# Projections of a two-layer graph network on one Trainium2 core: normalizing and turning the next 512 rows ahead of emptying the current products, and values before the weights' product

## The chip, the core and the metric

The kernel runs on one core of a Trainium2 chip. The metric is device time in microseconds (us) of one execution; the kernel before was timed three times. The engines go by the profile's names: PE is TensorE's matmul, PEld its weight load, DVE is VectorE, ACT is ScalarE, POOL is GpSimd, SP is SyncE, which here only issues transfers.

## What is computed

`x` has 4096 rows of 512, `adj` is a 4096 x 4096 matrix. Layer 0 is attention over all rows with the adjacency added to the scores; layer 1 is graph attention with 8 heads.

```python
h = relu(layernorm(x))
q, k, v = h @ Wq.T + bq, h @ Wk.T + bk, h @ Wv.T + bv
x = x + softmax(q @ k.T / sqrt(512) + adj + adj) @ v
h = relu(layernorm(x))
x = x + gat(h, adj)      # 8 heads of 64, masked softmax, elu
```

The change touches only how `h`, `v` and the queries of layer 0 are made. The kernel doesn't make `k`: it multiplies the two weights into one 512 x 512 matrix once (`a_sb`) and keeps a column `c_sb` from the query bias, so that the scores are a product of `h` with "queries" which already hold both weights.

## The kernel before, in words

`fast_path` has three stages: projections (pool `proj`, lines 168 to 260), attention of layer 0 (pool `attn`, 262 and following) and graph attention. A second path, taken only if a flag asks for it, plays no part here.

The projections start with loads: the first 512 rows of `x` by SyncE, then Wv, the bias rows, Wq and Wk by ScalarE's queue. The two weights share one buffer (`raw`, line 231), so Wk is loaded when Wq has been turned. Each is turned with 16 transposes on TensorE (line 237), four to one PSUM buffer (tag `pt`, two buffers), which ScalarE copies out (238). Their product takes 16 matmuls (242), the bias column 16 more with one moving column (250).

Then a loop over 8 sets of 512 rows (`NS`, lines 255 to 260), and in each turn:

- `load_x`: one transfer of 1 MB for the set after this one, into one of two `xt` buffers.
- `hidden`: the statistics of the four blocks of 128 rows on VectorE (156, 157), the reciprocal root through a power on GpSimd (144) and four small VectorE steps (145 to 148), the normalization in place (187), 16 transposes on TensorE into two `pt` buffers (194), and ScalarE's relu from there into `hT` (195).
- `values_of`: four products of four matmuls each into `mm` buffers (201; four of them), each emptied by VectorE, which adds the bias (205).
- `queries`: four more such products with the weights' product as stationary side (215), emptied and scaled by VectorE into `qs` (219), and a store of 1 MB to DRAM by SyncE (222).

float32 matmuls show as two in the profile, so the 16 matmuls of values are "x32" there.

Each engine works through its own queue in order. `seq(...)` keeps an instruction at its place in program order; where it is missing, a scheduler may place the instruction by its own judgement. In `hidden`, the VectorE work is under `seq`, the TensorE and ScalarE work is not; the emptying instructions at 205 and 219 aren't either. Waits between engines are semaphores that the framework sets where a tile is written or read.

When the last queries have been stored, the pool closes and the attention stage takes its space; its first loads (328, 266, 337) wait for that.

Of the kernel before, what the change touches and what calls it, by code (L numbers as in the profile page):

```python
# [10 lines left out]
F32 = mybir.dt.float32  # L11
BF16 = mybir.dt.bfloat16
AF = mybir.ActivationFunctionType
# [5 lines left out]
P = 128  # L19
N = 4096  # L20
D = 512
# [3 lines left out]
SB = 4  # L25
NS = NB // SB
KC = D // P
# [8 lines left out]
GC = 512  # L36
# [10 lines left out]
@with_exitstack  # L47
def adj_preln_gnn_kernel(
    ctx: ExitStack,
    tc: tile.TileContext,  # L50
    x: bass.AP,
    adj: bass.AP,
    wqT: bass.AP,
    bq: bass.AP,
    wkT: bass.AP,
    bk: bass.AP,
    wvT: bass.AP,
    bv: bass.AP,
    w1: bass.AP,
    a1T: bass.AP,  # L60
    a2T: bass.AP,
    a_ln: bass.AP,
    b_ln: bass.AP,
    out: bass.AP,
):
    nc = tc.nc
    keep = ctx.enter_context(tc.tile_pool(name="keep", bufs=1))
    flag = keep.tile([1, 1], mybir.dt.int32, name="flag")
    fast_path(
        tc, flag, x, adj, wqT, bq, wkT, bk, wvT, bv, w1, a1T, a2T, a_ln, b_ln, out  # L70
    )

    low = nc.values_load(flag[0:1, 0:1])
    with tc.If(low > 0):
        general_path(tc, x, adj, wqT, bq, wkT, bk, wvT, bv, w1, a1T, a2T, a_ln, b_ln, out)
# [3 lines left out]
def fast_path(  # L79
# [18 lines left out]
    nc = tc.nc  # L98
    seq = tc.keep_in_program_order
# [4 lines left out]
    ident = const.tile([P, P], F32, name="ident")  # L104
# [46 lines left out]
    def layernorm_stats(pool, rows, name):  # L151

        st = pool.tile([P, SB, 6], F32, name=f"{name}st", tag=f"{name}st", bufs=2)
        mv = pool.tile([P, SB, 2], F32, name=f"{name}mv", tag=f"{name}mv", bufs=2)
        for b in range(SB):
            seq(nc.vector.bn_stats(st[:, b, :], rows[b]))
            seq(nc.vector.bn_aggr(mv[:, b, :], st[:, b, :]))
        v = pool.tile([P, SB], F32, name=f"{name}v", tag=f"{name}v", bufs=2)
        seq(nc.vector.tensor_scalar_add(v, mv[:, :, 1], LN_EPS))
        return mv, rsqrt(pool, v, [P, SB], name)  # L160


    with tc.tile_pool(name="kv", bufs=1) as kv:
        hT = kv.tile([P, KC, N], F32, name="hT")
        v = kv.tile([P, NB, D], F32, name="v")


        with tc.tile_pool(name="proj_c", bufs=1) as pc, tc.tile_pool(
            name="proj", bufs=2
        ) as work, tc.tile_pool(name="proj_ps", bufs=2, space=PSUM) as psum:  # L170
            wv_sb = pc.tile([P, KC, D], F32, name="wv_sb")
            a_sb = pc.tile([P, KC, D], F32, name="a_sb")
            c_sb = pc.tile([P, KC], F32, name="c_sb")
            bq_sb = pc.tile([P, KC], F32, name="bq_sb")
            bv_sb = pc.tile([P, D], F32, name="bv_sb")

            def load_x(sb):
                xt = work.tile([P, SB, D], F32, name="xt", tag="xt", bufs=2)
                nc.sync.dma_start(
                    out=xt, in_=x[ts(sb, SB * P), :].rearrange("(c p) d -> p c d", p=P)  # L180
                )
                return xt

            def hidden(sb, xt):
                mv, rstd = layernorm_stats(work, [xt[:, b, :] for b in range(SB)], "h")
                for b in range(SB):
                    seq(nc.vector.tensor_scalar(
                        xt[:, b, :], xt[:, b, :], mv[:, b, 0:1], rstd[:, b : b + 1],
                        ALU.subtract, ALU.mult,
                    ))  # L190
                for k in range(KC):
                    pt = psum.tile([P, 512], F32, name="pt", tag="pt", bufs=2)
                    for b in range(SB):
                        nc.tensor.transpose(pt[:, ts(b, P)], xt[:, b, ts(k, P)], ident)  # L194
                    nc.scalar.activation(hT[:, k, ts(sb, GC)], pt, AF.Relu)

            def values_of(sb):
                for b in range(SB):
                    pv = psum.tile([P, 512], F32, name="pv", tag="mm", bufs=4)
                    for k in range(KC):  # L200
                        nc.tensor.matmul(  # L201
                            pv, hT[:, k, ts(sb * SB + b, P)], wv_sb[:, k, :],
                            start=k == 0, stop=k == KC - 1,
                        )
                    nc.vector.tensor_add(v[:, sb * SB + b, :], pv, bv_sb)


            half_scale = 0.5 / math.sqrt(D)

            def queries(sb):  # L210
                qs = work.tile([P, KC, GC], F32, name="qs", tag="qs", bufs=2)
                for o in range(KC):
                    pq = psum.tile([P, 512], F32, name="pq", tag="mm", bufs=4)
                    for k in range(KC):
                        nc.tensor.matmul(  # L215
                            pq, a_sb[:, k, ts(o, P)], hT[:, k, ts(sb, GC)],
                            start=k == 0, stop=k == KC - 1,
                        )
                    nc.vector.tensor_scalar(
                        qs[:, o, :], pq, c_sb[:, o : o + 1], half_scale, ALU.add, ALU.mult  # L220
                    )
                nc.sync.dma_start(out=q_d[sb], in_=qs)

            xts = {0: load_x(0)}
            nc.scalar.dma_start(out=wv_sb, in_=wvT.rearrange("(k p) o -> p k o", p=P))
            nc.scalar.dma_start(out=bv_sb, in_=bv[None, :].to_broadcast([P, D]))
            nc.scalar.dma_start(out=bq_sb, in_=bq.rearrange("(k p) -> p k", p=P))
            with tc.tile_pool(name="proj_a", bufs=1) as pa:
                turned = {}
                for name, w in (("q", wqT), ("k", wkT)):  # L230
                    raw = pa.tile([P, KC, D], F32, name="raw", tag="raw", bufs=1)
                    nc.scalar.dma_start(out=raw, in_=w.rearrange("(k p) o -> p k o", p=P))
                    turned[name] = pa.tile([P, KC, D], F32, name=f"w{name}_t")
                    for o in range(KC):
                        pt = psum.tile([P, 512], F32, name="pw", tag="pt", bufs=2)
                        for k in range(KC):
                            nc.tensor.transpose(pt[:, ts(k, P)], raw[:, k, ts(o, P)], ident)
                        nc.scalar.copy(turned[name][:, o, :], pt)
                for k in range(KC):
                    pa_ps = psum.tile([P, 512], F32, name="pa", tag="mm", bufs=4)  # L240
                    for o in range(KC):
                        nc.tensor.matmul(  # L242
                            pa_ps, turned["q"][:, o, ts(k, P)], turned["k"][:, o, :],
                            start=o == 0, stop=o == KC - 1,
                        )
                    nc.scalar.copy(a_sb[:, k, :], pa_ps)
                for e in range(KC):
                    pcb = psum.tile([P, 1], F32, name="pcb", tag="mm", bufs=4)
                    for o in range(KC):
                        nc.tensor.matmul(  # L250
                            pcb, turned["k"][:, o, ts(e, P)], bq_sb[:, o : o + 1],
                            start=o == 0, stop=o == KC - 1,
                        )
                    nc.vector.tensor_copy(c_sb[:, e : e + 1], pcb)
            for sb in range(NS):
                if sb + 1 < NS:
                    xts[sb + 1] = load_x(sb + 1)
                hidden(sb, xts.pop(sb))
                values_of(sb)
                queries(sb)  # L260

        with tc.tile_pool(name="attn", bufs=2) as work, tc.tile_pool(
            name="attn_ps", bufs=2, space=PSUM
# [6 lines left out]
            for t, a in ((aa[0], a1T), (aa[1], a2T)):  # L270
                nc.scalar.dma_start(
                    out=t.rearrange("p h e -> p (h e)"), in_=a[None, :].to_broadcast([P, D])
# [49 lines left out]
            raws, turned, probs, queries_of, sums, rows_of, totals = {}, {}, {}, {}, {}, {}, {}  # L322
# [262 lines left out]
    with tc.tile_pool(name="ga", bufs=2) as work, tc.tile_pool(name="ga_ps", bufs=2, space=PSUM) as psum:  # L585
# [187 lines left out]
        for k in range(NS):  # L773
            nX.append(gat.tile([P, SB, NH, HD], F32, name=f"nX{k}"))
            nc.scalar.dma_start(
                out=nX[k].rearrange("p b h e -> p b (h e)"),
                in_=nX_d[k * SB : (k + 1) * SB].rearrange("b p d -> p b d"),
# [457 lines left out]
```

## Time and profile before

The three runs took 4520.41, 4521.9 and 4522.26 us, median 4521.9. The profiled execution spans 4519.6 us.

| engine | busy us | share of the span |
|---|---|---|
| PE | 4147.6 | 92% |
| DVE | 2999.3 | 66% |
| ACT | 1899.9 | 42% |
| POOL | 1844.8 | 41% |

| stretch (us) | what | length | PE busy | PE clock |
|---|---|---|---|---|
| 0 to 47.04 | weights turned and multiplied | 47.04 | 24.79 | 0.99 |
| 47.04 to 86.36 | first 512 rows | 39.32 | 32.67 | 0.84 |
| 86.36 to 360.64 | seven more sets | 274.28 | 223.68 | 0.89 |
| 360.64 to 378.3 | last store, loads of the next stage | 17.66 | 1.09 | 0.59 |
| 378.3 to 2310 | attention | 1931.70 | 1931.66 | 1.00 |
| 2310 to 4519.6 | graph attention | 2209.60 | 1933.70 | 0.97 |

How to read it: the first table is a mean over stages, and can't say where TensorE waits. The second cuts the span by stage; the difference of length and busy is the time in which TensorE did nothing. "PE clock" is the share of TensorE's full clock that was granted. An engine that is idle costs time only where it is the one that the others wait for.

In the page, a digit in the 40 slices is the busy share in tenths. In the chain of waits each line is one piece of the work that ended last, followed back from the end; "issue" is time in which the engine waited for nothing that the profile shows. In the timeline, the bracket at the end of a line tells how long the engine stood idle before it and what released it.

### The profile page before, as it was taken

The page shows a single profiled execution, that of the slowest core. Times are in us where ns is not written, and L with a number is a line of the kernel's source. Part 1 is how long each engine was busy: PE and PEld are TensorE (multiplying, and loading weights), DVE is VectorE, ACT ScalarE, POOL GpSimd, SP SyncE. Part 2 cuts the span into 40 slices and gives each one's busy share as a digit, 9 for nine tenths or more (in the row PEclk, how much of TensorE's full clock was granted, in tenths as well). Part 3 has the DMA queues.
Part 4 walks back from the last instruction along what each step waited for, and adds up shares of the span by engine and source line. Part 5 has one row for each costly group of instructions (what it writes and reads, how often), then busy time and mean ns, then how long its engine had stood idle before and what let it go on. Part 6 is the DMA issues. An engine that isn't in the chain of part 4 may idle for free.

```text
span 4519.6 us, 44777 instructions
## 1 busy us (share of the span) xinstructions
PE 4147.6 (92%) x14738; PEld 1632.5 (36%) x14890; DVE 2999.3 (66%) x4369; ACT 1899.9 (42%) x1813; POOL 1844.8 (41%) x1494
## 2 busy tenths in 40 slices
PE   6888999999999999999992799999999999999997
PEld 3333444444444444444441222222222222222222
DVE  1232234444444444444444899999999999999998
ACT  1001111111111111111110677777777777777776
POOL 0001122222222222222222566666666666666665
PEclk9889999999999999999996899999999999999999
DMA  2103233333333333333322443434444444444332
GB/s 77 56 37 118 93 103 105 115 99 119 100 102 111 100 121 100 110 100 120 98 81 104 152 134 127 131 121 131 127 127 126 129 127 132 126 128 133 123 120 70
DMA packets 486416, 501.05 MB, mean 111 GB/s; under 512 B 42144, under 2 KB 355744, under 8 KB 485152
## 3 DMA queue, kind: packets, MB, share of 16 engines
q1 hardware_dynamic: 478592, 484.67, 33.2%
q10 hardware_dynamic: 7584, 13.44, 0.8%
q8 instruction: 119, 1.95, 0.2%
q14 instruction: 121, 0.99, 0.1%
HBM read 351.08 MB, written 146.93 MB: 110 GB/s over the span
## 4 chain that ended last, share of the span: by engine, by line
PE 51%; DVE 31%; issue 16%; DMA 1%; POOL 0%; ACT 0%; SPq 0%; ACTq 0%; DVEq 0%; POOLq 0%
PE ps L368 20%; PE acc L390 19%; DVE t L669 15%; DVE t L673 13%; PE m L443 3%; PE pv L201 3%; PE pt L353 2%; PE pq L215 2%; DVE t L679 1%; PE pt L194 1%; DVE y L729 0%; PE m L434 0%; DMA raw<-in_wqT_dram 0%; PE pa L242 0%; DMA nb<-nT_d 0%
## 5 line engine op out<-in xcount | busy, mean ns | idle before, releaser
L681 POOL TENSOR_TENSOR t<-t,g 128x1024 f32<-128x1024 f32 x512 | 1213.8, 2371 | 3.1 <-issue 3.1
L697 PE MATMUL acc<-t,nX 128*64 128x512 f32 x4096 | 1003.3, 611 | 6.9 <-ACT t L684 4.5
L684 ACT ACTIVATE t<-t 128x2048 f32<-128x2048 f32 x512 | 972.9, 1900 | 2.8 <-POOL t L681 2.8
L368 PE MATMUL ps<-qt,hT 128*128 128x512 f32 x2048 | 923.8, 594 | 0.0
L390 PE MATMUL acc<-v,p 128*128 128x512 f32 x2048 | 920.5, 592 | 0.0
L378 POOL TENSOR_TENSOR total<-total,p 128x512 f32<-128x512 f32 x248 | 317.4, 1280 | 1345.8 <-ACT p L373 1345.8
L661 ACT ACTIVATE t<-d 128x1024 f32<-128x1024 f32 x512 | 525.2, 1026 | 526.2 <-PE d L654 502.6
L669 DVE SCALAR_TENSOR_TENSOR t<-u,at2m,d 128x512 f32<-128x512 f32 x1024 | 713.1, 735 | 16.1 <-remote 16.1
L679 DVE TENSOR_TENSOR t<-t,g 128x1024 f32<-128x1024 f32 x512 | 645.1, 1260 | 15.1
L673 DVE TENSOR_TENSOR t<-t,d 128x1024 f32<-128x1024 f32 x512 | 618.0, 1207 | 0.6 <-ACT t L661 0.6
L357 DVE TENSOR_SCALAR ng<-aT 128x512 bf16<-128x512 f32 x256 | 125.2, 489 | 679.1 <-ACT aT L355 675.1
L390 PEld LDWEIGHTS acc<-v,p 128*128 128x128 f32 x2048 | 389.1, 190 | 489.8 <-issue 488.1
L373 ACT ACTIVATE p<-p 128x512 f32<-128x512 f32 x256 | 161.2, 630 | 958.2 <-DVE p L372 933.2
L649 PE MATMUL d<-z,z 6*128 6x512 bf16 x2048 | 386.6, 384 | 164.1 <-DVE t L669 139.9
L654 PE MATMUL d<-nb,ident_b 128*128 128x512 bf16 x1896 | 513.7, 383 | 13.3 <-issue 9.1
L368 PEld LDWEIGHTS ps<-qt,hT 128*128 128x128 f32 x2048 | 370.1, 191 | 369.2 <-issue 368.0
L697 PEld LDWEIGHTS acc<-t,nX 128*64 128x64 f32 x4096 | 250.1, 137 | 520.5 <-issue 463.9
L680 POOL TENSOR_TENSOR gate<-t 128x1 f32<-128x1 f32 x512 | 99.6, 194 | 729.2 <-DVE t L679 704.7
L372 DVE TENSOR_TENSOR p<-aT,ps 128x512 f32<-128x512 f32 x256 | 175.5, 685 | 293.4 <-PE ps L368 293.4
L649 PEld LDWEIGHTS <-z 6*128 6x128 bf16 x2048 | 94.8, 91 | 703.8 <-issue 684.1
L355 ACT COPY aT<-pt 128x512 f32<-128x512 f32 x256 | 149.7, 585 | 365.1 <-PE pt L353 320.9
L654 PEld LDWEIGHTS <-ident_b 128*128 128x128 bf16 x2048 | 158.7, 98 | 239.8 <-issue 119.5
(144 smaller groups left out, 2292.0 us busy)
## 6 DMA issues: line engine op xcount, KB each, us to landing
g<-gT_d SPq DMA_DIRECT2D x128, 1024.0 KB, 5.4
ag<-in_adj_dram SPq DMA_DIRECT2D x256, 256.0 KB, 2.8
gT_d<-gs SPq DMA_DIRECT2D x256, 256.0 KB, 2.0
nb<-nT_d SPq DMA_DIRECT2D x128, 512.0 KB, 3.2
nT_d<-ng SPq DMA_DIRECT2D x256, 128.0 KB, 2.1
z<-z_d SPq DMA_DIRECT2D x144, 128.0 KB, 2.0
xt<-in_x_dram SPq DMA_DIRECT2D x8, 1024.0 KB, 5.5
q_d<-qs SPq DMA_DIRECT2D x8, 1024.0 KB, 3.9
```

The lines of the kernel that those rows point to most:

```text
L368: seq(nc.tensor.matmul(ps, hT[:, k, ts(jt, P)], queries_of[ic][k], start=k == 0, stop=k == KC - 1))
L378: seq(nc.gpsimd.tensor_add(totals[ic], totals[ic], p))
L390: seq(nc.tensor.matmul(sums[ic][b], p[:, ts(b, P)], v[:, jt, :], start=jt == 0, stop=jt == NB - 1))
L649: seq(nc.tensor.matmul(pair[hh // 2][:, hh % 2, :], z2[rows, ts(jt % JB, P)], groups[ic, hg]["z1"][rows, :], start=True, stop=False,))
L654: seq(nc.tensor.matmul(pair[hh // 2][:, hh % 2, :], ident_b, ng[:, jt % JB, :], start=False, stop=True))
L661: seq(nc.scalar.activation(t[:, 0:2, :], zs[n][0], AF.Relu, scale=4.0))
L669: seq(nc.vector.scalar_tensor_tensor(t[:, 2 + e, :], u4[:, e, :], at2m[:, jt, h : h + 1], pair[1][:, e, :], ALU.max, ALU.add,))
L673: seq(nc.vector.tensor_add(t[:, 0:2, :], t[:, 0:2, :], pair[0]))
L679: seq(nc.vector.tensor_mul(t[:, 0:2, :], t[:, 0:2, :], g))
L681: seq(nc.gpsimd.tensor_mul(t[:, 2:4, :], t[:, 2:4, :], g))
L684: seq(nc.scalar.activation(logits[n], logits[n], AF.Exp))
L697: seq(nc.tensor.matmul(grp["acc"][hf][ts(e, HD), :], nX[jt // SB][:, jt % SB, hg * HG + 2 * hf + e, :], t[:, 2 * hf + e, :], start=jt == 0 ...
```

## The change

It moves work within the projections so that TensorE finds turned rows ready when it is through with the current products.

- `hidden` is split: `normalize` (statistics and normalization, VectorE and GpSimd) and `hidden` (transposes and relu). In the loop, the next set's `normalize` comes before the current set's values, and its `hidden` between values and queries.
- The first rows go first: `normalize`, `hidden` and `values_of` of set 0, then the weights' transposes, product and bias column, then `hidden` of set 1 and the queries of set 0.
- Wq and Wk get a raw buffer each and are loaded without waiting for each other's transposes.
- `load_x` makes four transfers of 256 KB, one for each 128 rows, so that a block's statistics wait for its own rows only.
- `qs` has one buffer in place of two.
- All instructions of the stage on TensorE, ScalarE and VectorE are now under `seq`.

```diff
             def load_x(sb):
                 xt = work.tile([P, SB, D], F32, name="xt", tag="xt", bufs=2)
-                nc.sync.dma_start(
-                    out=xt, in_=x[ts(sb, SB * P), :].rearrange("(c p) d -> p c d", p=P)
-                )
+                for b in range(SB):
+                    nc.sync.dma_start(out=xt[:, b, :], in_=x[ts(sb * SB + b, P), :])
                 return xt
 
-            def hidden(sb, xt):
+            def normalize(xt):
                 mv, rstd = layernorm_stats(work, [xt[:, b, :] for b in range(SB)], "h")
...
+            def hidden(sb, xt):
                 for k in range(KC):
                     pt = psum.tile([P, 512], F32, name="pt", tag="pt", bufs=2)
                     for b in range(SB):
-                        nc.tensor.transpose(pt[:, ts(b, P)], xt[:, b, ts(k, P)], ident)
-                    nc.scalar.activation(hT[:, k, ts(sb, GC)], pt, AF.Relu)
+                        seq(nc.tensor.transpose(pt[:, ts(b, P)], xt[:, b, ts(k, P)], ident))
+                    seq(nc.scalar.activation(hT[:, k, ts(sb, GC)], pt, AF.Relu))
...
-                qs = work.tile([P, KC, GC], F32, name="qs", tag="qs", bufs=2)
+                qs = work.tile([P, KC, GC], F32, name="qs", tag="qs", bufs=1)
...
-                turned = {}
+                raws, turned = {}, {}
                 for name, w in (("q", wqT), ("k", wkT)):
-                    raw = pa.tile([P, KC, D], F32, name="raw", tag="raw", bufs=1)
-                    nc.scalar.dma_start(out=raw, in_=w.rearrange("(k p) o -> p k o", p=P))
+                    raws[name] = pa.tile([P, KC, D], F32, name=f"w{name}_raw")
+                    nc.scalar.dma_start(out=raws[name], in_=w.rearrange("(k p) o -> p k o", p=P))
+                xts[1] = load_x(1)
+                normalize(xts[0])
+                hidden(0, xts.pop(0))
+                values_of(0)
+                normalize(xts[1])
+                for name in ("q", "k"):
                     turned[name] = pa.tile([P, KC, D], F32, name=f"w{name}_t")
...
-            for sb in range(NS):
+            hidden(1, xts[1])
+            queries(0)
+            for sb in range(1, NS):
                 if sb + 1 < NS:
                     xts[sb + 1] = load_x(sb + 1)
-                hidden(sb, xts.pop(sb))
+                    normalize(xts[sb + 1])
                 values_of(sb)
+                if sb + 1 < NS:
+                    hidden(sb + 1, xts[sb + 1])
                 queries(sb)
```

More of the change, by code (lines that the diff above doesn't have):

```diff
@@ L200, in values_of @@
                     for k in range(KC):
-                        nc.tensor.matmul(
+                        seq(nc.tensor.matmul(
                             pv, hT[:, k, ts(sb * SB + b, P)], wv_sb[:, k, :],
                             start=k == 0, stop=k == KC - 1,
-                        )
-                    nc.vector.tensor_add(v[:, sb * SB + b, :], pv, bv_sb)
+                        ))
+                    seq(nc.vector.tensor_add(v[:, sb * SB + b, :], pv, bv_sb))
             half_scale = 0.5 / math.sqrt(D)
             def queries(sb):
-                qs = work.tile([P, KC, GC], F32, name="qs", tag="qs", bufs=2)
+                qs = work.tile([P, KC, GC], F32, name="qs", tag="qs", bufs=1)
                 for o in range(KC):
@@ L214, in queries @@
                     for k in range(KC):
-                        nc.tensor.matmul(
+                        seq(nc.tensor.matmul(
                             pq, a_sb[:, k, ts(o, P)], hT[:, k, ts(sb, GC)],
                             start=k == 0, stop=k == KC - 1,
-                        )
-                    nc.vector.tensor_scalar(
+                        ))
+                    seq(nc.vector.tensor_scalar(
                         qs[:, o, :], pq, c_sb[:, o : o + 1], half_scale, ALU.add, ALU.mult
-                    )
+                    ))
                 nc.sync.dma_start(out=q_d[sb], in_=qs)
@@ L236, in fast_path @@
                         for k in range(KC):
-                            nc.tensor.transpose(pt[:, ts(k, P)], raw[:, k, ts(o, P)], ident)
-                        nc.scalar.copy(turned[name][:, o, :], pt)
+                            seq(nc.tensor.transpose(pt[:, ts(k, P)], raws[name][:, k, ts(o, P)], ident))
+                        seq(nc.scalar.copy(turned[name][:, o, :], pt))
                 for k in range(KC):
@@ L241, in fast_path @@
                     for o in range(KC):
-                        nc.tensor.matmul(
+                        seq(nc.tensor.matmul(
                             pa_ps, turned["q"][:, o, ts(k, P)], turned["k"][:, o, :],
                             start=o == 0, stop=o == KC - 1,
-                        )
-                    nc.scalar.copy(a_sb[:, k, :], pa_ps)
+                        ))
+                    seq(nc.scalar.copy(a_sb[:, k, :], pa_ps))
                 for e in range(KC):
@@ L249, in fast_path @@
                     for o in range(KC):
-                        nc.tensor.matmul(
+                        seq(nc.tensor.matmul(
                             pcb, turned["k"][:, o, ts(e, P)], bq_sb[:, o : o + 1],
                             start=o == 0, stop=o == KC - 1,
-                        )
-                    nc.vector.tensor_copy(c_sb[:, e : e + 1], pcb)
-            for sb in range(NS):
+                        ))
+                    seq(nc.vector.tensor_copy(c_sb[:, e : e + 1], pcb))
+            hidden(1, xts[1])
+            queries(0)
+            for sb in range(1, NS):
                 if sb + 1 < NS:
                     xts[sb + 1] = load_x(sb + 1)
-                hidden(sb, xts.pop(sb))
+                    normalize(xts[sb + 1])
                 values_of(sb)
+                if sb + 1 < NS:
+                    hidden(sb + 1, xts[sb + 1])
                 queries(sb)
```

## The prediction

> **What bounds the kernel now.** I read the page first: busy shares, then the 40 slices, because the shares are means over stages with different limits.
>
> ```profile
> PE   6888999999999999999992799999999999999997
> PEclk9889999999999999999996899999999999999999
> ```
>
> A slice is 4519.6 / 40 = 113 us. TensorE is full except in slices 1 to 4, the projections that the change touches, and around slice 21. Where TensorE is short of work its granted clock is lower too. Next, the chain of waits between 86 and 166 us, two turns of the loop over 512 rows (columns: start us, us, what):
>
> ```profile
> 86.36 6.74 issue
> 93.10 1.81 PE pt L194 x7
> 94.93 0.61 ACT hT L195
> 95.58 1.97 PE pt L194 x8
> 97.55 13.78 PE pv L201 x32
> 111.34 13.75 PE pq L215 x32
> 125.08 6.74 issue
> ...
> 136.27 14.90 PE pv L201 x32
> 151.17 13.75 PE pq L215 x32
> ```
>
> A turn is 13.8 to 14.9 us of values, 13.75 us of queries, and 11.2 us (86.36 to 97.55) in which TensorE waits and then turns rows round. The turns start at 86.36, 125.08 and 164.92, so they last 38.7 and 39.8 us. The label "issue" names nobody; the timeline of the gap does (start us, us, engine, line, operation):
>
> ```profile
> 86.38 0.75 DVE L219 TENSOR_SCALAR qs<-pq,c_sb 128x512 f32<-128x512 f32 x1 [2.68 <-PE pq L215]
> 87.05 0.68 DVE L156 BATCH_NORM_STATS2 hst<-xt 128x6 f32<-128x512 f32 x1
> ...
> 90.61 1.01 POOL L144 TENSOR_TENSOR hr<-hv,mhalf 128x4 f32<-128x4 f32 x1 [38.89 <-DVE hv L159]
> ...
> 92.45 1.91 DVE L187 TENSOR_SCALAR xt<-xt,hmv,hr 128x512 f32<-128x512 f32 x4
> 93.10 2.01 PE L194 MATMUL pt<-ident,xt 128*128 128x128 f32 x8 [6.76 <-issue]
> ```
>
> VectorE empties the last query product and only then starts the next rows' statistics, 4 of them, a power on GpSimd (1.01 us), four tiny steps and the normalization. TensorE's transposes begin 0.65 us after the first normalized block. The rows had long been loaded, so it is the place in VectorE's queue that makes the gap. The windows of the same stretch show what the gap does to the clock (columns: window, length, then busy us of PE, PEld, DVE, ACT, POOL, then PEclk):
>
> ```profile
> 86.36:97.55 11.19, 3.98 (x17) 3.12 (x18) 6.55 (x18) 1.68 (x3) 1.01 (x1) 0.69 0.23 94
> 97.55:111.34 13.79, 13.79 (x34) 6.14 (x33) 2.08 (x3) 0.60 (x1) 0.00 (x0) 1.00 0.21 77
> 111.34:125.08 13.74, 13.73 (x32) 5.72 (x31) 2.94 (x4) 0.00 (x0) 0.00 (x0) 1.00 0.00 0
> ```
>
> Last, the front and the price of a transpose at full clock, from the list of transfers in the first microsecond and the timeline of the attention stage:
>
> ```profile
> xt<-in_x_dram SPq DMA_DIRECT2D x1, 1024.0 KB, 8.6
> ```
>
> ```profile
> 465.54 0.60 PE L353 MATMUL pt<-ident,ag 128*128 128x128 f32 x4
> 465.97 3.60 PE L368 MATMUL ps<-qt,hT 128*128 128x512 f32 x8
> 466.23 0.59 ACT L355 COPY aT<-pt 128x512 f32<-128x512 f32 x1 [2.50 <-PE pt L353]
> ```
>
> Four transposes hold TensorE for 465.97 - 465.54 = 0.43 us there; ScalarE starts 0.69 us after the first of them and copies for 0.59 us.
>
> **What the Trainium skill says.** "TensorE: Matmul & The Clock Gate", Part 1 (the HAM clock gate): TensorE runs at half clock after about 3.4 us without work and needs about 3.4 us of work to come back. The trace agrees: in the 2 us windows 92 to 94 and 94 to 96, after the gap, the clock is 0.50, and 1.00 from 98 on. "PSUM — Partial Sum Buffer", Engine vs sequencer instructions: VectorE's queue is strict FIFO; the statistics at 87.05 behind the emptying at 86.38 agree. "Perfetto Trace Analysis", Matmuls: independent groups should rotate through banks so that emptying one overlaps the next. The products here have four buffers (tag mm); the trace shows queries following values with no gap (97.55 + 13.78 = 111.33, next start 111.34), so four hold.
>
> **The change part by part.** No product, statistic or copy is added or dropped. The instruction order of the changed build equals that of before on every engine from the first adjacency load on, so only the time up to the last query product, at 360.64 us on the chain, can move.
>
> *Steady turn.* In the new order VectorE does the next rows' normalization first, then 4 additions to v, then 4 query emptyings; TensorE does values, the next rows' transposes, queries. VectorE: the normalization lasts from 87.05 to 94.36 = 7.3 us (92.45 + 1.91), the additions 4 x 0.69 = 2.8, the emptyings 4 x 0.75 = 3.0, together 13.1 of some 30 us. It starts as the last query product is emptied, about 0.8 us into the turn, and ends at 8.1; TensorE wants the rows at 13.75. So it is hidden behind values, with 5.6 us to spare. The new wait: the additions queue behind the normalization on VectorE. Their four products fill the four buffers meanwhile (one each 3.44 us: ready at 3.4, 6.9, 10.3, 13.75); the first is emptied at 8.8, and the next taker of a buffer, the first query product, comes after 13.75 + transposes. Nobody waits.
>
> Transposes at full clock, two buffers (tag pt): groups 1 and 2 start at 0 and 0.43. ScalarE works from 0.69 to 1.29 (L195 is 0.60); group 3 starts at 1.34, ScalarE's second ends at 1.89, group 4 starts at 1.94 and leaves TensorE free at 2.37. This replaces 11.2 us. Bounds: 1.75 us if only 16 x 0.11 counts, and 4.4 if they stay at the cold rate (97.34 - 93.10 = 4.24, and a little). I take 2.37, as they follow 13.75 us of dense products. Turn: 13.75 + 2.37 + 13.75 = 29.9 us. Values too lose their cold start (14.9 becomes 13.75 in every second turn).
>
> *Front.* Before, TensorE starts at 16.6 on Wq's transposes, stands 5.6 us for Wk (its buffer is shared, so its load waits), and 6.2 us for the first normalization; queries of the first rows end at 86.36. After, the first rows come first. They landed at 0.74 + 8.6 = 9.3 us as one transfer; in four parts the statistics can start earlier, but the last part is taken at the same 9.3 (earliest some 7.4, since Wq and part of the next rows now wait for earlier transfers before they are issued). From the start of the last statistic (89.45) to the first transpose (93.10) are 3.65 us: start at 13.0. Cold transposes 4.24: 17.2. Values 14.4 (between 13.75 and 14.96): 31.6; Wv landed at 10.5. Wq and Wk now have their own buffers and arrive under this: five loads of 1 MB at the 340 to 400 GB/s of that stretch end at about 18. Their 8 groups of transposes, warm, by the same two-buffer count, 5.0: 36.6. The weights' product 13.75: 50.4. The bias product 3.75: 54.1. Next rows' transposes 2.4: 56.5. Queries 13.75: 70.3. That is 16.1 earlier than 86.36.
>
> *Sum.* Six full turns 6 x 29.9 = 179.2: 249.5. Last turn without transposes 27.5: 277.0. Before 360.64; saved 83.6 us. 4521.9 - 83.6 = 4438.3.
>
> *Edits at nothing.* Split loads: three more issues of about 0.4 us on SyncE per 512 rows, behind 30 us of products; they wait for the row buffer that transposes freed a turn earlier. One qs buffer in place of two: its store took 3.84 us in the chain (361.44 to 365.28), and the next writer comes 13.75 + 2.4 + 3.4 = 19.6 us after the last. In the new order on SyncE a store of queries stands behind a load of later rows; that load waits for transposes which TensorE does before those queries, so it is no detour. The end of the stage (last store, its loads, 360.64 to 378.3) keeps its waits.
>
> **The rivals.**
> 1. *The transposes break the clock.* With ScalarE's copies between them TensorE is busy 1.75 of 2.37 us, and half clock would mean 4.4 us for them and 14.9 for values: 7 x (2.0 + 1.15) = 22 us lost, 4460. For it: 0.50 beside transposes now. Against: that follows 6.74 idle us, and the attention stage mixes the same transposes with products at a clock of 1.00. 8%.
> 2. *VectorE's queue gives the gap back*, because rows come late or the additions hold products: then only the front's 16 us remain, 4506. Against: 5.6 us to spare, and loads of 5.5 to 13 us issued a turn ahead. 4%.
> 3. *Slower.* The single qs buffer and the mixed SyncE queue put store, load and normalization in a row on each turn: 3.8 + 5.5 + 7.3 = 16.6 us and 2.4 of transposes, against 11.2 now: +7.8 in 7 turns, +55, less the front's 16 and the warm values' 4: some 35 us more, 4557. For it: one buffer fewer, and the waits in SyncE's order. Against: the count above, where each wait is for something a turn old. 4%.
>
> **How the numbers follow.** The main case has 84%: 4438. Its bounds: rows at 7.4, -2; transposes at 1.75, -4; 4431 or so. Upwards: cold transposes alone +14, a late front +3: 4456. What lies outside is mostly rival 1's far end and rivals 2 and 3. Faster by 0.2% is below 4512.9: the main case and rivals 1 and 2, 0.94, some of rival 2 falling within; same 0.02; slower 0.04.
>
> **What would show it.** Right: turns of 29.9 us; transposes of about 2.4 us right behind the values; clock 1.00 from the second set of rows on; TensorE's first transpose at about 13; last query product at about 277; attention and the rest of unchanged length. Wrong: an idle TensorE ahead of the transposes with VectorE still in its statistics; a query product waiting for an addition; a clock of 0.5 within turns; or a later stage that has changed its length.

## The result

The changed kernel takes 4438.43 us (median of four runs, 4437.62 to 4439.83) against 4521.15 (4519.51 to 4522.26): a ratio of 0.9818, 95% interval 0.9801 to 0.9835, or 82.7 us less.

### The profile page after: what moved, and what is told of

Same layout as the page of the kernel before. It is cut to its first block, busy times and chain, and to the rows that moved or that the text cites. A ratio compares the mean times of both kernels' runs of the same rounds, so it can differ in the third digit from the quotient of the medians.

```text
span 4435.8 us, 44958 instructions
## 1 busy us (share of the span) xinstructions
PE 4142.4 (93%) x14890; PEld 1620.1 (37%) x14890; DVE 2999.3 (68%) x4369; ACT 1898.9 (43%) x1813; POOL 1845.0 (42%) x1494
## 4 chain that ended last, share of the span: by engine, by line
PE 52%; DVE 31%; issue 15%; DMA 1%; ACT 0%; POOL 0%; SPq 0%; ACTq 0%; DVEq 0%; POOLq 0%
PE ps L379 20%; PE acc L401 20%; DVE t L680 15%; DVE t L684 13%; PE m L454 3%; PE pt L364 3%; PE pv L202 2%; PE pq L216 2%; DVE t L690 1%; DVE y L740 0%; PE m L445 0%; PE pt L195 0%; PE pa L249 0%; DMA g<-gT_d 0%; POOL prod L485 0%
## 5 line engine op out<-in xcount | busy, mean ns | idle before, releaser
L665 PE MATMUL d<-nb,ident_b 128*128 128x512 bf16 x2048 | 534.2, 384 | 0.0
```

Of the source, the lines that this page charges most:

```text
L665: seq(nc.tensor.matmul(pair[hh // 2][:, hh % 2, :], ident_b, ng[:, jt % JB, :], start=False, stop=True))
```

## The profile after

The same two rows of the 40 slices, now of 4435.8 / 40 = 111 us each:

```profile
PE   8989999999999999999973999999999999999997
PEclk9999999999999999999985999999999999999999
```

Slices 1 and 3 hold an 8, for the wait at the front and for the close of the stage; the weak stretch of the turns is gone. The chain of waits over one turn (start us, us, what):

```profile
56.86 13.74 PE pq L216 x32
70.60 13.73 PE pv L202 x32
84.33 0.45 PE pt L195 x4
...
84.80 0.61 ACT hT L196
...
85.45 1.15 PE pt L195 x8
86.60 13.73 PE pq L216 x32
```

From queries to queries 86.60 - 56.86 = 29.74 us, where it was 38.7 and 39.8. Between values and queries stand 2.27 us of transposes (84.33 to 86.60). VectorE's timeline shows why they find their rows ready:

```profile
71.30 0.68 DVE L156 BATCH_NORM_STATS2 hst<-xt 128x6 f32<-128x512 f32 x1
...
76.71 1.91 DVE L186 TENSOR_SCALAR xt<-xt,hmv,hr 128x512 f32<-128x512 f32 x4
78.54 1.28 DVE L206 TENSOR_TENSOR v<-pv,bv_sb 128x512 f32<-128x512 f32 x2
```

The statistics still follow the last query emptying, but TensorE is in its values meanwhile. The normalization ends at 78.6, 5.7 us before the transposes want it; the two products that waited for it are then emptied in a row. The window over the transposes has the clock at full speed (columns as in the prediction: after the window its length, the busy us of the five engines, then PEclk, here 1.00):

```profile
84.33:86.60 2.27, 2.02 (x17) 1.71 (x16) 0.69 (x1) 1.54 (x3) 0.00 (x0) 1.00 0.00 0
```

Where the time went, from the chains and stage windows of both kernels:

| stretch | before | after |
|---|---|---|
| to the end of set 0's queries | 86.36 | 70.60 |
| seven more sets | 274.28 | 205.90 |
| to attention's first score product | 18.8 | 18.7 |
| on to the same transposes late in attention (at 2292.28 and 2207.42) | 1912.8 | 1912.2 |
| from there to the end of the span | 2227.3 | 2228.4 |

15.8 us come from the front and 68.4 from the turns. The later stages keep their lengths to within about 1 us.

## The experiments

The theory: a turn got shorter because VectorE's queue holds the next normalization ahead of the emptyings, so that it lies beside the values. Rivals: it is the new place of the transposes on TensorE; it is the clock, which the idle time cooled; it is the new front, or the split loads.

### The front alone

```diff
 # set 1 as in the changed kernel, then:
-                    normalize(xts[sb + 1])
+                if sb > 1:
+                    normalize(xts[sb])
+                    hidden(sb, xts[sb])
                 values_of(sb)
-                if sb + 1 < NS:
-                    hidden(sb + 1, xts[sb + 1])
                 queries(sb)
```

> The new front alone: from set 2 on, a turn is normalization, transposes, values, queries as before. Queue theory (the gain of the turns comes from VectorE doing the next normalization before the emptyings): the front ends at 70.6 us as in the changed kernel, turn 1 takes 27.5, six turns take 39.3 each again: last query product near 334, time 4438 + 57 = 4495. Rival (the front and its warm clock are most of the gain): below 4460.

Measured: 4496.79 us (4494.52 to 4497.54), ratio 0.9948 (0.9931 to 0.9965). On the chain the last query product ends at 334.0.

### The turns alone

```diff
 # weights first, one raw buffer, as before the change; then:
+            normalize(xts[0])
+            hidden(0, xts[0])
-            for sb in range(1, NS):
+            for sb in range(NS):
```

> The new turns alone: weights first with one raw buffer and the wait for Wk, then set 0, as before. Queue theory: queries of set 0 end at 86.4 + 2.3 = 88.7, then 6 x 29.73 + 27.5: last query product at 294.5, time 4438 + 18 = 4456. Rival (front is most of the gain): above 4490.

Measured: 4452.94 us (4451.64 to 4453.98), ratio 0.9849 (0.9833 to 0.9866); last query product at 293.0. It came out 3 us below the expectation: TensorE began on Wq at 15.43, not at 16.64 as before, probably since the later parts of the second set's rows are now issued late (the last of the eight at 9.4 us), and so leave more of the transfer engines to Wq; no run isolates this.

Both together: the front alone takes 360.6 - 334.0 = 26.6 us off the last query product, the turns alone 67.6. The sum is 94.2, the change's own 84.1. The difference of 10.1 is in the main one turn's gap, which each of the two removes for set 1: a turn of the kernel before lasted 274.28 / 7 = 39.2 us in the mean, so 39.2 - 29.7 = 9.5 were lost in each. So the front is not most of it.

### Normalization late, transposes in their new place

```diff
-                    normalize(xts[sb + 1])
                 values_of(sb)
                 if sb + 1 < NS:
+                    normalize(xts[sb + 1])
                     hidden(sb + 1, xts[sb + 1])
```

> The changed kernel, but in the loop the next normalization stands behind the emptying of the values; the transposes stay between values and queries. Queue theory: TensorE stands 6.7 us between values and transposes, transposes and the next products are cold again: six turns of 39.3 instead of 29.73, 4495. Rival (it is the place of the transposes on TensorE that counts): 4438 to 4445.

Measured: 4495.84 us (4494.86 to 4496.72), ratio 0.9946 (0.9929 to 0.9962). The chain of this kernel:

```profile
84.41 0.69 DVE v L206
85.10 0.61 DVE hst L156
...
91.11 4.41 PE pt L195 x16
95.53 14.70 PE pq L216 x32
```

The gap of before is back whole, between values and queries: VectorE's emptying at 84.41, then its statistics, transposes 6.7 us later and cold at 4.41 us, the next product cold at 14.70. One move in VectorE's queue decides 57 us. Nor is it `seq` that made the gain, since this kernel has it everywhere and loses the turns' share.

### Transposes late, normalization ahead

```diff
                 values_of(sb)
-                if sb + 1 < NS:
-                    hidden(sb + 1, xts[sb + 1])
                 queries(sb)
+                if sb + 1 < NS:
+                    hidden(sb + 1, xts[sb + 1])
```

> The changed kernel, but the next set's transposes come after the queries, right before the values that need them; the normalization stays ahead. Queue theory: TensorE finds normalized rows in either place, and values need the last turned quarter only 2.6 us after they start, so the place costs nothing: 4438, at most 0.3 us more in each of 6 turns, 4440. Rival (place of the transposes counts): values wait for ScalarE and a good part of the 84 us is lost, 4455 or more.

Measured: 4439.8 us (4438.87 to 4441.51), ratio 0.9822 (0.9805 to 0.9838). Its turns last 29.74 us on the chain (101.80 to 131.53). The place of the transposes costs nothing that these runs resolve; this rival is out.

### The gap kept, the clock kept warm

```diff
 # the kernel before, and after queries(sb) in each turn but the last:
+                    idle = psum.tile([P, 512], F32, name="idle", tag="idle", bufs=1)
+                    for k in range(7):
+                        seq(nc.tensor.matmul(
+                            idle, a_sb[:, k % KC, 0:P], hT[:, k % KC, ts(sb, GC)],
+                            start=k == 0, stop=k == 6,
+                        ))
```

TensorE's instructions are under `seq` here, in the same order as before.

> The kernel before, with seven matmuls that nobody reads (6.0 us at full clock) on TensorE in each of the seven gaps of 6.74 us between queries and the next transposes. They add work and change no data. Queue theory: the normalization still has to be waited for, but the clock stays at 1.00, so the transposes take some 3.4 us behind the normalized blocks instead of 4.45 and values 13.75 instead of 14.3 in the mean: 1.7 us a turn, 12 us in all, about 4509. Clock theory (the cold clock is most of what the gap costs): 40 us or more, below 4480. If only the bubble counts: 4521.

Measured: 4511.14 us (4509.03 to 4512.66, 11 runs), ratio 0.9977 (0.9968 to 0.9986): 10.4 us less with 7 x 6 us of work added. TensorE's timeline in the gap, and the window over it:

```profile
85.03 6.17 PE L264 MATMUL idle<-hT,a_sb 128*128 128x512 f32 x14
91.95 2.09 PE L194 MATMUL pt<-ident,xt 128*128 128x128 f32 x8 [0.75 <-PE idle L264]
```

```profile
85.23:95.43 10.20, 8.84 (x31) 4.30 (x30) 6.55 (x18) 1.54 (x3) 1.01 (x1) 1.00 0.25 104
```

The clock stays at 1.00 here (in one of the seven gaps it fell for 3.41 us, from 207.83), the transposes take 3.48 us (91.95 to 95.43) behind the single normalized blocks, the values 13.73. The turn is 37.7 us (from 71.46 to 109.17). So of the 9.5 us that a turn lost by the change, the clock is 39.2 - 37.7 = 1.5 (seven times that is the 10.4 us by which the medians differ), the wait for the first normalized block 6.7, and the rest, about 1.2, the wait of the first transposes for the blocks after it. The clock theory is out as the main cause, and in as a sixth of it.

### One raw buffer, two query buffers

```diff
-                    raws[name] = pa.tile([P, KC, D], F32, name=f"w{name}_raw")
+                    raws[name] = pa.tile([P, KC, D], F32, name="raw", tag="raw", bufs=1)
...
+                    if name == "k":
+                        load_w("k", wkT)
...
-                qs = work.tile([P, KC, GC], F32, name="qs", tag="qs", bufs=1)
+                qs = work.tile([P, KC, GC], F32, name="qs", tag="qs", bufs=2)
```

> The changed kernel with one raw buffer shared by Wq and Wk, as before, and two qs buffers, as before. My theory: Wk's load is issued only when Wq's transposes are done, at about 35 us, lands 5.4 us later, TensorE stands for it: 4438 + 5.5 = 4444; the second qs buffer changes nothing in the turns (29.73). Rival (one qs buffer costs something): turns below 29.73 and the time at or below 4438.

Measured: 4445.52 us (4444.43 to 4446.49), ratio 0.9832 (0.9816 to 0.9849). On the chain Wk's load takes 5.56 us from 35.39 on, and the turns are 29.74 us (96.61 to 126.35) with two query buffers too. The weights' product begins at 44.48, where it began at 37.33 in the changed kernel. So the second raw buffer is worth some 7 us; the second query buffer is worth nothing. No run has two of both; whether they would fit is not shown.

### One transfer for each set of rows

```diff
-                for b in range(SB):
-                    nc.sync.dma_start(out=xt[:, b, :], in_=x[ts(sb * SB + b, P), :])
+                nc.sync.dma_start(
+                    out=xt, in_=x[ts(sb, SB * P), :].rearrange("(c p) d -> p c d", p=P)
+                )
```

> The changed kernel with one transfer of 1 MB for each set of rows, as before. My theory: only the first set is waited for, all four statistics follow its landing at 9.3 us, TensorE starts at 15.4 instead of 13.9: 4440, turns unchanged at 29.73. Rival (split loads keep the later turns fed): turns get longer, 4450 or more.

Measured: 4438.85 us (4436.17 to 4441.35), ratio 0.9818 (0.9802 to 0.9835). TensorE's first transpose is at 15.09, not 13.88; turns are 29.74. The split is worth 1.2 us on the chain, less than the runs scatter.

### More work on VectorE ahead of the normalization

```diff
                     xts[sb + 1] = load_x(sb + 1)
+                    for _ in range(6):    # 16 in the second kernel
+                        spare = work.tile([P, D], F32, name="spare", tag="spare", bufs=1)
+                        seq(nc.vector.tensor_add(spare, bv_sb, bv_sb))
                     normalize(xts[sb + 1])
```

> The changed kernel with six additions of 128x512 that nobody uses (about 0.67 us each, 4.0 together) on VectorE ahead of the normalization in each of six turns. By the slack of 5.6 us: no change, 4438. If VectorE already set the pace: 6 x 4 = 24 us more, 4462.

Measured: 4438.98 us (two runs, 4438.86 and 4439.1), turns of 29.74. Some 4 us more of VectorE in each turn are hidden.

> The same with sixteen additions (10.7 us) in each of six turns. By the slack of 5.6 us: the normalization ends 5.1 us after the values, TensorE stands about 4 us and waits for single blocks, turns of about 34.8, or 36 if the clock falls: 4468 to 4477. If VectorE set the pace: 6 x 10.7 = 64 us more, 4502. If it never matters: 4438.

Measured: 4485.26 us (two runs, 4482.6 and 4487.92), above the expected range. One turn by windows:

```profile
88.04:92.58 4.54, 0.00 (x0) 0.03 (x1) 3.18 (x12) 0.00 (x0) 1.01 (x1) 0.96 0.00 0
92.58:97.00 4.42, 4.42 (x17) 3.29 (x18) 3.62 (x7) 1.79 (x3) 0.00 (x0) 0.50 0.00 0
97.00:111.83 14.83, 14.83 (x33) 6.49 (x33) 2.25 (x3) 0.60 (x1) 0.00 (x0) 0.93 0.22 71
```

TensorE stands 4.54 us, and then the transposes run at a clock of 0.50 and take 4.42 instead of 2.27, the queries 14.83 instead of 13.74. A turn is 37.5 us: 7.8 more, of which 4.5 are the wait and 3.2 what follows from it. Not all of the 3.2 is the clock: with the clock at 1.00 in the gap above, transposes behind single blocks took 3.48 us too, so some 0.9 of their 4.42 and the 1.1 of the queries are. An addition took 0.73 us from start to start, not 0.67, so 16 of them are 11.6 us. The slack is confirmed by the pair: 4 us are free, 11.6 leave a gap of 4.5, and the arithmetic 11.6 + 8.1 - 1.3 - 13.75 = 4.6 gives the same (normalization ends at 8.1, the first block is ready 1.3 before that).

### The last turn swapped

The chain of the changed kernel ends the stage with a store of the last queries:

```profile
276.52 0.76 DVE qs L220
...
277.30 3.85 DMA q_d<-qs
```

```diff
                 if sb + 1 < NS:
...
+                else:
+                    queries(sb)
+                    values_of(sb)
```

> The changed kernel, but in the last turn the queries come before the values, so that their store (3.85 us, alone on the chain before the stage closes) runs beside the last values. Theory (the store is on the path): 3.9 us less, 4434.5. Rival (the loads of the next stage are bound by something else): 4438.

Measured: 4435.03 us (4433.91 to 4436.73, five runs), ratio 0.981 (0.9796 to 0.9823). In its chain an emptying of values is followed directly by the next stage's load, with no store:

```profile
280.22 0.70 DVE v L206
...
281.07 6.39 DMA w_sb<-in_w_dram
```

In the changed kernel that load starts 4.98 us after the last product (276.50 to 281.48), here 0.87 (280.20 to 281.07). That is 4.1 us; the medians differ by 3.4.

### Wq first

```diff
 # on top of the swap; Wq's load is issued first on its queue, and:
+                turn_w("q")
                 normalize(xts[0])
                 hidden(0, xts.pop(0))
                 values_of(0)
                 normalize(xts[1])
+                turn_w("k")
```

> As the one with the last turn swapped, and Wq is loaded first on its queue and turned before the first rows, while VectorE normalizes these. Theory: Wq lands at about 10.5, its transposes fill TensorE until the first rows are normalized at 13.9, and 2.4 us of them no longer follow the values: 4432. Rival (it delays the first rows by sharing the transfer engines, or the transposes by ScalarE's copies): 4434.5 or more.

Measured: 4430.78 us (4430.47 to 4431.66, five runs), ratio 0.9801 (0.9788 to 0.9814). The last product ends at 275.0 (280.2 before this edit, in an execution with the slow front of the next section). Against the changed kernel's own profile the weights' product begins 2.8 us earlier (34.51, 37.33). It beats both kernels: its five runs lie below all four of the changed kernel, by 7.7 us in the median. The two were measured beside the same kernel before, but not beside each other.

### The bias product spread

In the traces the front is not always the same. The changed kernel's chain has set 0's queries at 56.86, for 13.74 us (shown above); the one with the swapped last turn has the lines below, and both ran the same instructions up to there:

```profile
55.95 3.61 PE pt L195 x16
59.56 14.73 PE pq L216 x32
```

```diff
 # on top of Wq first: inside the loop over the weights' product
                     seq(nc.scalar.copy(a_sb[:, k, :], pa_ps))
-                for e in range(KC):
                     pcb = psum.tile([P, 1], F32, name="pcb", tag="mm", bufs=4)
...
```

> As the one with Wq first, and the bias column's product (16 matmuls with one moving column, 3.5 us in one piece) is spread: four of them behind each quarter of the weights' product. In several profiled runs the clock fell to 0.50 around that piece, the next transposes took 3.6 us instead of 2.3 and the next queries 14.7 instead of 13.74. If the piece of one-column matmuls makes the clock fall: transposes of set 1 at about 2.3 and queries of set 0 at 13.74 here, 1 to 3 us less, 4428 to 4430. If something else does: 4430.8 as before and the cold times remain possible.

Measured: 4430.44 us (4429.23 to 4431.18, five runs), ratio 0.9799 (0.9786 to 0.9813). Its profile has the clock at 1.00 throughout that stretch and set 0's queries at 13.74, but the median moved by 0.3 us only, inside the scatter. One warm profile is what chance can give, too.

The times at which the clock changes say more. Read in windows of 0.1 us, in stretches of all the traces, they lie whole multiples of 3.413 us apart within an execution. In the kernel before they are 46.33, 59.98, 90.70, 97.53, 128.25 and 138.49: distances of 4, 9, 2, 9 and 3 such steps. So a low stretch is whole steps long, and this is why values took 14.9 us in every second turn there: the clock stayed low for 3 steps (10.24 us) in those turns and for 2 (6.83) in the others. Where the points lie differs from execution to execution. Ten profiled executions, the changed kernel's among them, ran the bias product in one piece right before set 1's transposes. Sorted by the first such point after that product began (where the clock kept still nearby, carried back from later changes):

| first point after the start (us) | profiled executions | clock at 0.50 for |
|---|---|---|
| 0.72 to 1.74 | Wq first, front alone, transposes late | 3.41 us |
| 1.87 to 2.00 | normalization late, one transfer, the changed kernel | not at all |
| 2.65 to 2.85 | 6 and 16 additions, last turn swapped, one raw buffer | 6.83 us |

In the last group the clock falls inside the product, though TensorE has no gap there (the swapped last turn, from the product's start):

```profile
51.91:54.61 2.70, 2.70 (x27) 2.70 (x26) 0.41 (x3) 0.58 (x1) 0.00 (x0) 1.00 0.00 0
54.61:61.44 6.83, 6.83 (x26) 5.39 (x27) 0.22 (x2) 2.39 (x4) 0.00 (x0) 0.50 0.11 26
```

In the first group it falls one step later, among the transposes, 0.7 to 1.7 us after the product's end. So the cold fronts belong to the product in one piece, and how much is lost hangs on where the points lie. With the product spread, one piece would have begun at 34.13 + 13.74 = 47.87 and the next point is at 50.67, 2.80 us later: the third group's place, and yet the clock stayed up. This speaks for the spreading, on one execution; what it is worth in the median is not resolved, and why one-column matmuls let the clock fall stays open.

## Why the prediction was right

The time of 4438.43 lies 0.1 us from the 4438.3 that was predicted. That it is so close is luck, as the terms show: by the chain, 84.1 us were saved where the working had 83.6; by the medians it is 82.7, against a kernel before that came out 0.75 us below the 4521.9 that the working started from.

- *The gap is VectorE's order.* Right, and shown from both sides: moving only the normalization back gives 4495.84, moving only the transposes back changes nothing.
- *The steady turn.* 29.9 predicted, 29.74 measured. Transposes 2.27 instead of 2.37, products 13.73 instead of 13.75. The two-buffer count held: the third group starts when ScalarE has emptied the first (84.80 + 0.61, 85.45).
- *VectorE hidden with 5.6 us to spare.* Measured 5.7 on the timeline; confirmed with 4 us added (nothing) and with 11.6 (a gap of 4.5).
- *The new wait costs nobody anything.* Right: two products waited in their buffers until 78.54, and no product of TensorE started late.
- *Front.* 70.3 predicted, 70.60 measured in that profile. Single terms were off by up to 0.9 and cancelled: the start is 13.88, not 13.0, because the third part of the rows landed only at 9.3 and the fourth soon after, so the last statistic began at 10.16; values 14.11 for 14.4, the bias product 3.47 for 3.75. In another profiled execution the front is 3.7 us longer, 2.8 of it from the bias product on, where the transposes and the queries run cold; the working had no term for that. Its "cold" 4.24 for the first transposes was right in size (4.41, as long as those at 0.50 in the kernel with the late normalization), although the clock column reads 1.00 there, as it did for the weights' stretch before: this column seems to show nothing ahead of the clock's first change.
- *Edits at nothing.* Split loads and the single query buffer: right. The order of stores and loads on SyncE made no wait in any turn.
- *Rival 1 (clock).* In the turns the clock stayed at 1.00, as the attention stage had suggested. What a low clock would have cost is shown by the kernel with 16 additions: about 0.9 for transposes and 1.1 for the product after each gap of 4.5 us. There it was the gap that brought it; no turn shows transposes alone doing so.
- *Rivals 2 and 3.* Neither happened: rows were there, and turns didn't grow.
- The close of the stage kept its waits, as the working had it; that the store in it could be hidden was not seen in the prediction.

## What to carry to other kernels

Where the busiest engine has a gap that repeats once in a loop and the timeline shows another engine starting its preparation only after its last emptying, move that preparation ahead in that engine's queue, and count two things: the slack until it is wanted, and the buffers that must hold what now waits behind it. In this kernel it then hardly mattered where the busiest engine did the preparation's last step. At the end of a stage, put the product whose result must be stored first, so that its store runs beside the other.

## What was not expected

- A gap of 4.54 us on TensorE cost 7.8: the transposes after it took 4.42 instead of 2.27 us and the product 14.83 instead of 13.74, at clocks of 0.50 and 0.93. "TensorE: Matmul & The Clock Gate", Part 1 of the Trainium skill, has about 3.4 us without work as the bound; the gap of 4.54 us agrees, and the expectation should have used it in full.
- The same instructions at the front took 3.7 us more in one profiled execution (set 0's queries end at 74.29 with the swapped last turn) than in another (70.60). Of this, 2.8 us arise from the bias product on (4.04, 3.61 and 14.73 us for it, the transposes and the queries, against 3.47, 2.33 and 13.74). The clock fell there without a gap on TensorE, and where its 3.413 us steps lay decided for how long.
